# Two recurrent layers: where the gate's mixing product and the per-head mean of the output are computed

## The chip, the core and the metric

The program runs on one core of one Trainium2 chip. The core has five engines that each work through their own queue in order and wait for one another by semaphores: TensorE (PE, matrix products, with weight loads shown apart as PEld), VectorE (DVE), ScalarE (ACT), GpSimd (POOL) and SyncE (SP, which only issues transfers). [...] The metric is the device time of one execution in microseconds (us), as a median over several runs.

## What is computed

Four layers run one after the other on four sequences of 512 rows of 512 channels, all in 32-bit floats: a cross attention, two recurrent layers of the RWKV kind and a last attention with an MLP. The change lies in the two recurrent layers. Cut to what matters, one of them is:

```python
xn = ln(x); sx = shifted(xn) - xn
t  = tanh((xn + sx * maa_x) @ maa_w1).reshape(b, l, 5, 32)
m  = einsum('blfd,fdc->blfc', t, maa_w2)          # five of them: w k v r g
xw, xk, xv, xr, xg = (xn + sx * (maa_j + m_j) for each j)
w  = exp(-exp(time_decay + tanh(xw @ decay_w1) @ decay_w2))
r, k, v = xr @ Wr.T, xk @ Wk.T, xv @ Wv.T ;  g = silu(xg @ Wg.T)
# per head (32 heads of 16 channels), for each row in turn:
#   a = k^T v ; out = r (u * a + s) ; s = a + w * s
gm = mean(y over the 16 channels of a head)
gv = mean((y - gm)**2 over the same)
y  = (y - gm) * rsqrt(gv + eps) * gn_w + gn_b
x  = x + (y * g) @ Wo.T
# then a channel mix of its own (layer norm, two shifted inputs, three products)
```

## The kernel before

**Units.** Each recurrent layer is cut into pieces of 256 rows of one sequence: 2 layers x 4 sequences x 2 halves make 16 units, numbered q. In a unit the recurrence takes eight steps (two halves e of the value channels times four channel groups i). A global step counter g runs over all units, eight steps for each. Products of later units and the output and channel work of earlier ones are laid between the steps, so that three or four units are in work at a time.

**Order.** The order of the instructions on PE, DVE, ACT and POOL is the order in which the program text issues them; nothing rearranges it within these layers. The loop over g issues, at each step: `summed(g-1)` (PE adds up the products of the last step, `py`), `begun(g+1)` (DVE multiplies keys and values into `kv` and `A`, and POOL issues a transfer that adds `A` to `kv` in SBUF), `scan(g)` (the DVE scan along time, and two DVE products `ry`), perhaps `repeated` (PE spreads values into `vr`), and then four phases EARLY, SOON, MID, LATE. Into these phases the generators `mixes(q)`, `outputs(q)` and `channels(q)` put their pieces: a `yield 9, LATE` means "go on in the LATE phase of step 9, counted from the unit's own first step". Within one phase the order is that in which the pieces were registered. At the end of MID every fourth step has `taken`, where DVE adds `py` to half of `y`.

**Buffers.** `A` has one buffer: the product that fills it for step g+1 must wait for the transfer of step g. The small products share three PSUM buffers (tag `p`), the mixing inputs four SBUF buffers (tag `mix`, in turn for `mixx`, `mix_w`, `mix_k`, `mix_v`, `mix_r`, `mix_g`, `ruk`). `mean` and the later `bc` share one.

**The pieces that are touched.** In `mixes`, the helper `second(pair)` computes the second mixing product for one or two of the five letters. For w, k, v, r the weights lie in 32-row strips of one tile; those of g lie in rows 64 to 96 of the tile `dw2`, under the decay's second matrix in rows 0 to 64. `second("g")` is called alone, in the LATE phase of step -5, after `product("k")`; the decay's own second product is in the EARLY phase of step -5. ACT then takes each from PSUM: for g with an Identity and a bias (L665), for the decay with an Exp (L744). `mixed("g")` at step -4, LATE, multiplies by the shift on DVE (L671) and adds the unshifted input by a transfer from POOL (L584).

In `outputs`, the mean over a head's 16 channels starts at step 9, EARLY. The channels of a head lie on four partitions times four slots, and `gmean` is a constant matrix of 1/16 for partitions of one head; four products over the four slots of `y` add up in one PSUM tile, ACT copies it out (L907), and DVE subtracts it (L909). Then come the squares on ACT (L912), the variance on PE (L917) and DVE (L927), its power -1/2 on POOL (L929), and the scaling. What stands next to these in the same phases belongs to other units: at step 8, LATE, that is step 0 of the next unit, where POOL computes `y = v * al` (L799) and `y + rk` (L800) for it.

Of the kernel before, what the change touches and what calls it, by code (L numbers as in the profile page):

```python
# [8 lines left out]
F32 = mybir.dt.float32  # L9
I32 = mybir.dt.int32  # L10
AF = mybir.ActivationFunctionType
ALU = mybir.AluOpType
# [3 lines left out]
P = 128  # L16
B, L, C = 4, 512, 512
KC = C // P
LT = L // P
HS = 16  # L20
TS = 256
BUFS = {"mix": 4, "cx": 3}
# [8 lines left out]
def tile_xattn_rwkv_perceiver(ctx: ExitStack, tc: tile.TileContext, t: dict, out: bass.AP):  # L31
    nc = tc.nc
# [38 lines left out]
    def mm(ps, pairs):  # L71
        for i, (lhsT, rhs) in enumerate(pairs):
            nc.tensor.matmul(ps, lhsT, rhs, start=(i == 0), stop=(i == len(pairs) - 1))  # L73
# [22 lines left out]
    def psum_tile(shape, name):  # L96
        pool, tag = psum["p"]
        return pool.tile(shape, F32, tag=tag, name=name)
# [356 lines left out]
    def recurrent(lp, ep):  # L455
        NI = 4
# [5 lines left out]
        EARLY, SOON, MID, LATE = range(4)  # L462

        mp = sp = pvr = pyp = W = A = None
# [19 lines left out]
        gmean = lp.tile([P, P], F32, name="gmean")  # L484
# [41 lines left out]
        def perm(w, i):  # L526

            return w.rearrange("p (m i) -> p i m", i=NI)[:, i]
# [4 lines left out]
        def pairs(a):  # L533

            return a.rearrange("p i (m o) -> p i o m", o=2)
# [57 lines left out]
        def mixes(q):  # L593
# [5 lines left out]
            c = small[li]  # L599
            vec, order = c["vec"], orders[li]  # L600
# [14 lines left out]
            else:  # L615
                both = wpool.tile([P, 2, KC, TS], F32, tag="w", name="sx0")
                sx, mix = both[:, 0], both[:, 1]
            shift(sx, cur, stT[:, :, b, 1] if hf == 0 else st[q - 1]["last"])
            yield (-10, EARLY) if q == 1 else (-9, LATE)
            if mp:  # L620
                mix = mp.tile([P, KC, TS], F32, tag="mix", name="mixx", bufs=BUFS["mix"])
# [5 lines left out]
            th = lp.tile([P, 2, TS], F32, tag="th", name="th")  # L627
            pm = psum_tile([P, TS], "pm")
            mm(pm, [(c["w1"][:, k, :P], mix[:, k, :]) for k in range(KC)])
            nc.scalar.activation(th[:, 0, :], pm, AF.Tanh)  # L630
            pm = psum_tile([P, TS], "pm")
            for k in range(KC):
# [4 lines left out]
                    start=(k == 0),  # L637
                    stop=(k == KC - 1),
                    tile_position=(0, 64),
                )  # L640
            nc.scalar.activation(th[64:96, 1, :], pm[64:96], AF.Tanh)
            ms = {}

            def second(pair):

                for x in pair:
                    ms[x] = mp.tile([P, KC, TS], F32, tag="mix", name="mix_" + x, bufs=BUFS["mix"])
                for k in range(0, KC, 2):
                    pms = {x: psum_tile([P, 2, TS], "pmm") for x in pair}
                    for a in range(2):  # L650
                        for x in pair:
                            f = order.index(x)
                            r, w = (32 * f, c["w2"]) if f < 4 else (64, c["dw2"])
                            nc.tensor.matmul(
                                pms[x][:, a, :],
                                w[r : r + 32, (k + a) * P : (k + a + 1) * P],
                                th[r : r + 32, f // 4, :],
                                start=True,
                                stop=True,
                                tile_position=(r, 0),  # L660
                            )
                    for x in pair:
                        i = V_MAA + order.index(x)
                        for a in range(2):
                            nc.scalar.activation(  # L665
                                ms[x][:, k + a, :], pms[x][:, a, :], AF.Identity, bias=vec[:, k + a, i : i + 1]
                            )
# [64 lines left out]
            pm = psum_tile([P, TS], "pm")  # L732
            mm(pm[:64], [(c["dw1"][:, k], ms["w"][:, k, :]) for k in range(KC)])
            td = sp.tile([64, TS], F32, tag="td", name="td", bufs=1)
            nc.scalar.activation(td, pm[:64], AF.Tanh)
            mixed("vr")
            yield -5, EARLY
            w = d["w"] = mp.tile(full, F32, tag="o_w", name="o_w", bufs=1)
            for i in range(0, NI, 2):
                pm = psum_tile([P, 2, TS], "pm")  # L740
                for a in range(2):
                    mm(pm[:, a, :], [(perm(c["dw2"][:64], i + a), td)])
                for a in range(2):
                    nc.scalar.activation(  # L744
                        w[:, i + a, :].rearrange("p (o m) -> p o m", o=2),
                        pairs(pm)[:, a],
                        AF.Exp,
                        bias=c["vk"][:, i + a, V_DECAY : V_DECAY + 1],
                    )
            nc.scalar.activation(w, w, AF.Exp, scale=-1.0)  # L750
            yield -5, MID
            product("k")
            yield -5, LATE
            second("g")
            yield -4, MID
            if q > 0:
                product("v")
# [30 lines left out]
            pm = psum_tile([P, TS + TP], "al")  # L788
# [9 lines left out]
            y = d["y"] = mp.tile(full, F32, tag="y", name="y")  # L798
# [97 lines left out]
        def outputs(q):  # L896

            li, b, hf = units[q]
            n = f"L{li}_"
            c, d = small[li], st[q]  # L900
            y = d["y"]
            NQ = TS // 4
            full = [P, NI, TS]
            pm = psum_tile([P, TS], "pmean")
            mm(pm, [(gmean, y[:, i, :]) for i in range(NI)])
            mean = sp.tile([P, TS], F32, tag="mean", name="mean", bufs=1)
            nc.scalar.copy(mean, pm)  # L907
            yield 9, LATE
            nc.vector.tensor_tensor(y, y, mean[:, None, :].to_broadcast(full), ALU.subtract)  # L909
            yield 10, EARLY  # L910
            sq = mp.tile(full, F32, tag="cx", name="sq", bufs=BUFS["cx"])
            nc.scalar.activation(sq, y, AF.Square)  # L912
            yield 10, SOON
            var = psum_tile([P, NQ], "var")
            for i in range(NI):
                for a in range(4):
                    nc.tensor.matmul(  # L917
                        var[32 * a : 32 * a + 32],
                        gm32,
                        sq[:, i, NQ * a : NQ * a + NQ],  # L920
                        start=(i == 0),
                        stop=(i == NI - 1),
                        tile_position=(0, 32 * a),
                    )
            yield 10, LATE
            rstd = sp.tile([P, NQ], F32, tag="gn_rs", name="gn_rs")
            nc.vector.tensor_scalar(rstd, var, 1.0, 1e-5, ALU.mult, ALU.add)  # L927
            yield 11, EARLY
            nc.gpsimd.tensor_tensor(rstd, rstd, mhalf[:, :NQ], ALU.pow)  # L929
            yield 12, LATE  # L930
            for a in range(4):
                rs = slice(32 * a, 32 * a + 32)
                nc.scalar.copy(rp[rs, NQ * a : NQ * a + NQ], rstd[rs])
            yield 13, EARLY
            pm = psum_tile([P, TS], "pbc")
            mm(pm, [(gself, rp)])
            bc = sp.tile([P, TS], F32, tag="mean", name="bc", bufs=1)
            nc.scalar.copy(bc, pm)
            yield 13, LATE
            nc.vector.tensor_tensor(y, y, bc[:, None, :].to_broadcast(full), ALU.mult)  # L940
            yield 14, EARLY

            yg = mp.tile(full, F32, tag="cx", name="yg", bufs=BUFS["cx"])
            for i in range(NI):
                nc.scalar.activation(
                    yg[:, i].rearrange("p (m o) -> p o m", o=2),
                    y[:, i].rearrange("p (o m) -> p o m", o=2),
                    AF.Identity,
                    bias=c["gn"][:, i, 1:2],
                    scale=c["gn"][:, i, 0:1],  # L950
                )
            nc.gpsimd.tensor_tensor(yg, yg, d["g"], ALU.mult)
            yield 15, MID
            wo = wpool.tile([P, NI, C], F32, tag="w", name=n + "wo")
            for a in range(4):
                nc.sync.dma_start(
                    wo[32 * a : 32 * a + 32], t[n + "Wo"].rearrange("(h a i) n -> a h i n", a=4, i=NI)[a]
                )
            pms = []
            for lt in range(NT):  # L960
                pm = psum_tile([P, C], "pm")
                mm(pm, [(yg[:, i, lt * P : (lt + 1) * P], wo[:, i, :]) for i in range(NI)])
                pms.append(pm)
            yield 15, LATE
            for lt in range(NT):
                x = xn[b][hf * NT + lt]
                nc.vector.tensor_tensor(x, pms[lt], x, ALU.add)
# [76 lines left out]
        def follow(q, at, gen):  # L1044
            g, ph = at
            steps.setdefault((G * q + g, ph), []).append((q, gen))

        follow(0, at, first)
        for q in range(len(units)):
            if q > 0:  # L1050
                follow(q, (-13 if q == 1 else -11, LATE), mixes(q))
            follow(q, (9, EARLY), outputs(q))
            follow(q, (19, LATE), channels(q))
        end = G * len(units)
        with (
# [419 lines left out]
```

## Time and profile before

| what | value |
|---|---|
| median of 3 runs | 3840.64 us |
| lowest and highest | 3837.99 and 3846.04 us |
| the profiled execution's own time | 3843.51 us |
| its span, first to last instruction | 3841.5 us |
| instructions in the span | 52407 |
| busy PE, PEld | 3589.6 us (93%), 1900.9 us (49%) |
| busy DVE, ACT, POOL | 2765.4 us (72%), 1691.6 us (44%), 1768.4 us (46%) |
| mean granted PE clock | 0.965 |
| four mean products, all units (L73 pmean) | 128 records, 33.7 us busy on PE |
| the gate's second product, 15 units (L654 pmm<-th,L_dw) | 120 records, 29.8 us |
| the decay's second product, 15 units (L73 pm<-td,L_dw) | 120 records, 33.5 us |
| DVE waiting at L833 for the transfer kv<-A | 88.0 us in 41 waits |
| DVE waiting at L909 for ACT's copy of the mean | 30.8 us in 13 waits |

A product of 32-bit floats shows as two records in the profile, so four products are eight records. The busy time of PE is a union of records that overlap. The recurrent layers fill the stretch from about 760 to 2420 us; the attention layers lie before and after it. An idle time is written in brackets with the instruction that ended it; an engine that is idle is only a cost where it is late for somebody else.

### The profile page before, as it was taken

What the parts mean: (1) busy time and instruction counts of PE and PEld (TensorE: products, weight loads), DVE (VectorE), ACT (ScalarE), POOL (GpSimd) and SP (SyncE); (2) the same over time, 40 slices, a digit from 0 to 9 for tenths busy, and PEclk for the clock granted to TensorE, in tenths of its full rate; (3) what the DMA queues carried; (4) which work ended last, traced back from release to release, by engine and by line L of the source; (5) the groups of instructions that cost most, each with busy time, mean ns of one, the idle gap of its engine ahead of it and who ended that gap; (6) DMA issues with size and microseconds to landing.
All of it is one profiled execution on the core that took longest, in us unless ns stands there. A gap on an engine that the chain in (4) does not pass through costs nothing.

```text
span 3841.5 us, 52407 instructions
## 1 busy us (share of the span) xinstructions
PE 3589.6 (93%) x20544; PEld 1900.9 (49%) x20544; DVE 2765.4 (72%) x4665; ACT 1691.6 (44%) x2514; POOL 1768.4 (46%) x834
## 2 busy tenths in 40 slices
PE   9999999988899999999999967899999999999989
PEld 3333333455565665655665634444454444544446
DVE  6777777689988888888888871388655665667531
ACT  4777676533444444444444422133343334324531
POOL 4777777424444444444444432065533433444430
PEclk9999999989999999999999988899999999999999
DMA  4000000166677777777777754200022122121223
GB/s 149 23 12 23 12 9 20 51 143 133 146 168 176 180 182 171 178 172 167 170 170 171 176 126 129 69 28 17 31 90 70 58 65 71 59 67 36 91 93 121
DMA packets 188805, 386.66 MB, mean 101 GB/s; under 512 B 18128, under 2 KB 44880, under 8 KB 186512
## 3 DMA queue, kind: packets, MB, share of 16 engines
q1 hardware_dynamic: 150256, 251.72, 20.8%
q0 software_dynamic: 38304, 131.61, 18.5%
q8 instruction: 162, 2.65, 0.3%
q14 instruction: 83, 0.68, 0.1%
HBM read 247.50 MB, written 4.19 MB: 66 GB/s over the span
## 4 chain that ended last, share of the span: by engine, by line
PE 64%; DVE 15%; DMA 6%; issue 5%; POOL 5%; ACT 5%; SPq 0%; POOLq 0%; DVEq 0%; ACTq 0%
PE pm L73 9%; PE pv L73 6%; PE po L73 5%; DMA kv<-A 5%; PE ph L73 5%; PE psc L242 5%; PE pst L279 4%; PE pst L1175 3%; PE psc L1175 3%; PE po L304 3%; PE pr L73 3%; DVE ry L867 3%; PE pk L73 3%; PE po L1235 2%; DVE kv L862 2%
## 5 line engine op out<-in xcount | busy, mean ns | idle before, releaser
L1230 POOL TENSOR_TENSOR acc<-acc,aT 128x2048 f32<-128x2048 f32 x96 | 435.0, 4531 | 420.4 <-ACT aT L1225 235.6
L292 POOL TENSOR_TENSOR aT<-aT,nmT 128x1536 f32<-128x1536 f32 x124 | 428.6, 3461 | 206.8 <-ACT aT L290 183.4
L254 DVE CUSTOM_DVE_ANT_0 sc<-psc,nm 128x512 f32<-128x512 f32 x512 | 354.0, 691 | 147.0 <-PE psc L242 89.3
L1220 DVE TENSOR_TENSOR aT<-pst,mb 128x512 f32<-128x512 f32 x512 | 317.4, 681 | 132.0 <-PE pst L1175 132.0
L867 DVE TENSOR_TENSOR ry<-kv,o_r 128x1024 f32<-128x1024 f32 x256 | 347.7, 1398 | 3.5
L862 DVE TENSOR_TENSOR_SCAN kv<-W,kv 128x1032 f32<-128x1032 f32 x128 | 296.1, 2313 | 0.2 <-DMA kv<-A 0.2
L584 POOL DMA_DIRECT2D kv<-A x127 | 118.9, 936 | 379.9 <-DVE kv L839 376.8
L290 ACT COPY aT<-pst 128x512 f32<-128x512 f32 x372 | 196.4, 595 | 178.2 <-PE pst L279 177.7
L298 ACT ACTIVATE aT<-aT 128x2048 f32<-128x2048 f32 x128 | 246.7, 1929 | 5.7 <-POOL aT L292 4.9
L73 PE MATMUL po<-l_m,hT 128*128 128x512 f32 x512 | 237.0, 606 | 9.2 <-ACT hT L1320 9.0
L73 PE MATMUL ph<-nT,l_m 128*128 128x256 f32 x1024 | 240.7, 391 | 0.0
L73 PEld LDWEIGHTS ph<-nT,l_m 128*128 128x128 f32 x1024 | 195.1, 194 | 64.9 <-issue 27.2
L1228 POOL TENSOR_TENSOR acc<-aT 128x2048 f32<-128x2048 f32 x16 | 72.4, 4524 | 327.6 <-ACT aT L1223 327.6
L833 DVE TENSOR_TENSOR A<-vr,o_k 128x1024 f32<-128x1024 f32 x128 | 155.6, 1216 | 88.1 <-DMA kv<-A 88.0
L279 PE MATMUL pst<-q,km 32*128 32x512 f32 x1024 | 206.2, 639 | 9.4 <-DVE mxs L254 5.8
L1189 DVE CUSTOM_DVE_ANT_0 sc<-psc,zeros,mx 128x512 f32<-128x512 f32 x256 | 177.5, 746 | 50.7 <-PE psc L1175 48.4
L1225 ACT ACTIVATE aT<-aT 128x2048 f32<-128x2048 f32 x64 | 122.3, 1911 | 196.6 <-DVE aT L1220 191.6
L1223 ACT ACTIVATE aT<-aT,mc 128x2048 f32<-128x2048 f32 x64 | 128.2, 2003 | 180.3 <-DVE aT L1220 171.0
L242 PE MATMUL psc<-km,q 32*128 32x512 f32 x1024 | 198.8, 653 | 0.8 <-ACT q L223 0.8
L881 PE MATMUL py<-ry,k 128*32 128x512 f32 x1024 | 158.5, 626 | 42.4 <-DVE ry L867 29.6
L929 POOL TENSOR_TENSOR gn_rs<-gn_rs,mhalf 128x64 f32<-128x64 f32 x16 | 186.4, 11648 | 23.0 <-DVE gn_rs L927 23.0
L1189 DVE CUSTOM_DVE_ANT_0 sc<-psc,nm 128x512 f32<-128x512 f32 x256 | 162.9, 686 | 46.5 <-PE psc L1175 45.0
(266 smaller groups left out, 7189.9 us busy)
## 6 DMA issues: line engine op xcount, KB each, us to landing
l_m<-in_L_W SPq DMA_DIRECT2D x64, 1024.0 KB, 5.1
kv<-A POOLq DMA_DIRECT2D x127, 516.0 KB, 7.4
L_wk<-in_L_Wk SPq DMA_DIRECT2D x16, 1024.0 KB, 8.0
L_wr<-in_L_Wr SPq DMA_DIRECT2D x16, 1024.0 KB, 7.8
L_wv<-in_L_Wv SPq DMA_DIRECT2D x16, 1024.0 KB, 6.0
L_wg<-in_L_Wg SPq DMA_DIRECT2D x16, 1024.0 KB, 7.8
L_wo<-in_L_Wo SPq DMA_DIRECT2D x64, 256.0 KB, 7.5
L_fk<-in_L_fWk SPq DMA_DIRECT2D x16, 1024.0 KB, 8.3
```

The lines of the kernel that those rows point to most:

```text
L73: nc.tensor.matmul(ps, lhsT, rhs, start=(i == 0), stop=(i == len(pairs) - 1))
L242: nc.tensor.matmul(psc, d["q"][g][rs, lt * P : (lt + 1) * P], d["km"][rs, a, :], start=True, stop=True, tile_position=(32 * r, 0),)
L254: nc.vector.tensor_tensor_reduce(sc, ps[r], d["nm"][lt], 1.0, -3.0e38, ALU.add, ALU.max, mxs[:, a, lt, c : c + 1])
L279: nc.tensor.matmul(pst, d["km"][rs, a, s * P : (s + 1) * P], d["q2", a][rs, :], start=True, stop=True, tile_position=(32 * r, 0),)
L292: nc.gpsimd.tensor_tensor(w[:, n:, :], w[:, n:, :], nmT[:, None, :].to_broadcast([P, NR - n, L]), ALU.add)
L298: nc.scalar.activation(w, w, AF.Exp)
L862: nc.vector.tensor_tensor_scan(flat(kv), flat(W[g % 2]), flat(kv), 0.0, ALU.mult, ALU.add)
L867: nc.vector.tensor_tensor(y, kv[:, 4 * h : 4 * h + 4, None, :TP].to_broadcast([P, 4, 2, TP]), d["r"][:, i].rearrange("p (o m) -> p o m", o ...
L1175: nc.tensor.matmul(psc, lhsT[rs], rhs[rs], start=True, stop=True, tile_position=(32 * r, 0))
L1189: nc.vector.tensor_tensor_reduce(sc, ps[r], d["nm"][a], 1.0, mx[:, 0, lt, r : r + 1] if a else 3.0e38, ALU.add, ALU.min, mx[:, a, lt, r : ...
L1220: nc.vector.tensor_tensor(w[:, r, :], ps[r], d["mb"][:, r, :], ALU.subtract)
L1230: nc.gpsimd.tensor_tensor(d["acc", m], d["acc", m], w, ALU.add)
```

## The change

Three edits.

First, in `mixes`, the gate's second product is taken out of its own place (step -5, LATE, after the key product) and written into the loop of the decay's second product (step -5, EARLY). For each of two passes there are now two PSUM tiles, `pm` for the decay and `pmm` for the gate, and PE gets a decay product in rows 0 to 64 of the array, then a gate product in rows 64 to 96, twice. ACT takes the decay's two halves, then the gate's two halves, in each pass. The yield at step -5, LATE, is gone with the call; `product("v")`, or `product("r")` in the first unit, stays at step -4, MID.

Second, in `outputs`, POOL adds the four slots of `y` into `mean`, and PE multiplies that sum by `gmean` once. The first add, of the two slots that are complete after step 4, comes at step 6, LATE; the two others at step 8, LATE, after the `taken` of that step; the product stays at step 9, EARLY.

Third, the generator `outputs` is started at step 6, LATE, in place of step 9, EARLY, for that.

In POOL's order the first add follows the scaling and shift of the units before and precedes a kv<-A issue; the two others precede L799 and L800 of the next unit. The orders of DVE and SP are as they were (one of SP's transfers of `wo` changes places with two small weight loads, once), ACT's and PE's differ only in the instructions named.

```diff
+            mg = ms["g"] = mp.tile([P, KC, TS], F32, tag="mix", name="mix_g", bufs=BUFS["mix"])
+            ig = V_MAA + order.index("g")
             for i in range(0, NI, 2):
-                pm = psum_tile([P, 2, TS], "pm")
+                pm, pmg = psum_tile([P, 2, TS], "pm"), psum_tile([P, 2, TS], "pmm")
                 for a in range(2):
-                    mm(pm[:, a, :], [(perm(c["dw2"][:64], i + a), td)])
+                    nc.tensor.matmul(
+                        pm[:, a, :], perm(c["dw2"][:64], i + a), td, start=True, stop=True, tile_position=(0, 0)
+                    )
+                    nc.tensor.matmul(
+                        pmg[:, a, :],
+                        c["dw2"][64:96, (i + a) * P : (i + a + 1) * P],
+                        th[64:96, 1, :],
+                        start=True,
+                        stop=True,
+                        tile_position=(64, 0),
+                    )
...
+                for a in range(2):
+                    nc.scalar.activation(mg[:, i + a, :], pmg[:, a, :], AF.Identity, bias=vec[:, i + a, ig : ig + 1])
             nc.scalar.activation(w, w, AF.Exp, scale=-1.0)
             yield -5, MID
             product("k")
-            yield -5, LATE
-            second("g")
             yield -4, MID
...
+            mean = sp.tile([P, TS], F32, tag="mean", name="mean", bufs=1)
+            nc.gpsimd.tensor_tensor(mean, y[:, 0, :], y[:, 1, :], ALU.add)
+            yield 8, LATE
+            for i in range(2, NI):
+                nc.gpsimd.tensor_tensor(mean, mean, y[:, i, :], ALU.add)
+            yield 9, EARLY
             pm = psum_tile([P, TS], "pmean")
-            mm(pm, [(gmean, y[:, i, :]) for i in range(NI)])
-            mean = sp.tile([P, TS], F32, tag="mean", name="mean", bufs=1)
+            mm(pm, [(gmean, mean)])
             nc.scalar.copy(mean, pm)
...
-            follow(q, (9, EARLY), outputs(q))
+            follow(q, (6, LATE), outputs(q))
```

## The prediction

> **What bounds the kernel now.** The page gives 93% to PE and 72% to DVE over the whole span. The change touches the recurrent layers only, so I read the busy time there, in hundreds of microseconds (columns: stretch, its length, then busy us and instruction count of PE, PEld, DVE, ACT, POOL, the granted clock, DMA share, GB/s).
>
> ```profile
> 1600.00:1700.00 100.00, 94.95 (x647) 60.40 (x649) 87.40 (x91) 46.36 (x92) 46.45 (x32) 1.00 0.73 169
> ```
>
> PE leads, but DVE is only 7 us behind. An average of that kind cannot say which of two engines paces, so I took the timeline of one unit (half a batch of one layer, eight scan steps, about 98 us). First VectorE (start, duration, operation, and in brackets its idle time and what ended it):
>
> ```profile
> 1631.35 4.33 DVE L867 TENSOR_TENSOR ry<-kv,o_r 128x1024 f32<-128x1024 f32 x2
> 1636.21 0.68 DVE L894 TENSOR_TENSOR y<-py,y 128x512 f32<-128x512 f32 x1
> 1636.81 1.21 DVE L833 TENSOR_TENSOR kv<-vr,o_k 128x1024 f32<-128x1024 f32 x1
> 1637.94 1.21 DVE L833 TENSOR_TENSOR A<-vr,o_k 128x1024 f32<-128x1024 f32 x1
> 1639.07 0.16 DVE L839 COPY kv<-S 128x8 f32<-128x8 f32 x1
> 1639.14 2.29 DVE L862 TENSOR_TENSOR_SCAN kv<-W,kv 128x1032 f32<-128x1032 f32 x1
> 1641.47 2.36 DVE L867 TENSOR_TENSOR ry<-kv,o_r 128x1024 f32<-128x1024 f32 x2
> 1645.15 1.23 DVE L909 TENSOR_TENSOR y<-y,mean 128x1024 f32<-128x1024 f32 x1 [1.32 <-ACT mean L907]
> 1649.70 1.22 DVE L833 TENSOR_TENSOR A<-vr,o_k 128x1024 f32<-128x1024 f32 x1
> 1658.18 0.23 DVE L927 TENSOR_SCALAR gn_rs<-var 128x64 f32<-128x64 f32 x1 [0.32 <-PE var L917]
> 1681.04 0.69 DVE L894 TENSOR_TENSOR y<-py,y 128x512 f32<-128x512 f32 x1 [3.94 <-PE py L881]
> 1688.01 1.22 DVE L833 TENSOR_TENSOR A<-vr,o_k 128x1024 f32<-128x1024 f32 x1 [4.01 <-DMA kv<-A]
> ```
>
> DVE waits for PE three times: 1.32 us before the subtraction of the mean, 0.32 us for the variance, 3.94 us at L894. The third is worth nothing: two instructions later DVE waits 4.01 us more for the kv<-A transfer, whose issue stands on POOL behind the power of L929:
>
> ```profile
> 1629.97 3.49 POOL L799 TENSOR_TENSOR y<-o_v,al 128x1024 f32<-128x1024 f32 x1
> 1636.43 1.27 POOL L800 TENSOR_TENSOR y<-y,rk 128x512 f32<-128x512 f32 x1 [2.96 <-DVE rk L794]
> 1639.53 0.87 POOL L584 DMA_DIRECT2D kv<-A  x1 [1.83 <-DVE kv L839]
> 1661.61 11.72 POOL L929 TENSOR_TENSOR gn_rs<-gn_rs,mhalf 128x64 f32<-128x64 f32 x1
> 1677.13 1.53 POOL L584 DMA_DIRECT2D kv<-A  x1
> ```
>
> So in this unit the pace is: PE up to the variance, then power, transfer and DVE until the next unit. DVE has no bracket over 0.6 us between 1688 and the next 1.5 us wait for the mean at 1744. In 4 of the 12 middle units (their gate step at 1027, 1127, 1321 and 1417 us) DVE waits 2.9 to 3.8 us for ACT o_g at L717; ACT there follows PE's receptance product, so PE paces those units throughout. In the first units (before 1000 us) DVE has no wait for the mean.
>
> The PE rows that the change touches:
>
> ```profile
> 1642.72 1.99 PE L73 MATMUL pmean<-y,gmean 128*128 128x256 f32 x8
> 1667.98 2.23 PE L73 MATMUL pm<-td,L_dw 64*128 64x256 f32 x8
> 1677.91 1.99 PE L654 MATMUL pmm<-th,L_dw 32*128 32x256 f32 x8
> ```
>
> **Mean, on PE.** Four products (8 records) become one. The step from pmean's start to the next row's is 1.92 us; a quarter stays, 0.48, so 1.44 us goes per unit, ahead of the variance and hence on PE's path.
>
> **Mean, on POOL.** Three adds of 128x256 appear. Price: L1230 adds 128x2048 in 4531 ns, L800 adds 128x512 in 1272 ns; the line through both is 187 ns + 2.12 ns per element, so 0.73 us each. Below nothing it cannot be; if the cost did not shrink from 512 elements it is 1.27. I take 0.73. The first add stands in POOL's order behind the shift of L588/L589 and ahead of a kv<-A issue that idles 2.1 us for DVE (3.8 in other units): hidden. The other two are put ahead of L799 and L800 of the next unit, which in turn stand ahead of the kv<-A issue at 1639.53. And they wait for L894, so everything behind them on POOL now begins at L894's end.
>
> **What that wait does to DVE.** Row first: while L799 runs, DVE's ry pair takes 4.33 us; the next pair takes 2.36. Here L799 costs DVE 1.97 us. [...] L833 reads vr from PSUM and keeps its 1.21 us everywhere. [...] the two adds fall beside the two L833.
>
> Count from L894's end (t). L799 no longer runs beside ry, so t comes 1.97 us earlier than before. Adds 0.15 to 1.6. L799 takes 2.38 us (its undisturbed minimum), 1.6 to 4.0. DVE's two L833 last to 2.27, then the copy L839 is held to 4.0. L800 takes its turn, to 5.4 (in the trace the engines alternate: L589, queued behind L588, waits for one ry and not for two). Scan 5.4 to 7.7, ry to 9.95. Against the old t that is 7.98; before, L909 began at 8.26. So DVE is held 2.9 us where it was held 1.97, and the 1.32 us wait for the mean is gone: 0.28 us gained. ACT's mean copy is then ready some 0.9 us earlier (the W copy before it becomes the limit), and PE, which reaches pmean 5.8 us after the old t, finds the adds long done. PE's variance is 1.44 us earlier, so the 0.32 us wait falls too: **0.6 us per unit** where DVE and POOL pace. The kv<-A issue moves from 2.63 to 3.5 after the old t; a landing takes 7.4 us, so at 1647.8, before 1649.4 when the next A wants the buffer. That transfer costs nothing, with 1.6 us left.
>
> **Gate beside the decay, on PE.** Eight records of the gate leave their place between key and value products and are laid between the decay's eight. Nearest row: the other maa pair (L654, two row groups interleaved) takes 1.56 + 1.13 us and a wait of 0.59 for ACT to free one of three PSUM buffers, 3.2 us in all; the new step has the same four tiles, buffers and waits. Before: 2.16 + 1.92 = 4.08. I take 3.4, the decay's strided weights being slower to load, so 0.7 us goes. [...] the other end is a loss of 0.6, if nothing overlaps and the wait comes on top. All of it lies after the variance, beside the power and the 11 us transfer, so it counts only in PE-paced units. ACT does the same evacuations, four of them earlier, before exp; nothing reads o_w for over 20 us. Should that cover go, it is under 2 us per unit. mix_g takes mix_w's buffer, already read. DVE's order is unchanged.
>
> **Sum.** Eight DVE-paced units: 8 x 0.6 = 4.8. Four PE-paced: 4 x (1.44 + 0.7) = 8.6, DVE's wait at L717 leaving room. Three early units without a wait to remove: about +0.9 each for two of them, -1.9 in all. Last unit, where pmean stands in the chain of waits: 1.4. First, where the gate's products do: 0.7. Together 13.6 us from the profiled run's 3843.5: 3829.9. That run lies 2.9 above the median of 3840.64, so I forecast **3827**; its own range, adds at 0.55 to 0.9 us, is 3818 to 3836. 0.2%, or 7.7 us, is about what a measurement can tell from no change.
>
> **Rivals.**
> 1. PE paces everywhere (for: its 95%; against: DVE's waits for transfers). Fifteen units at 2.1 us less: 3840.6 - 32 = 3809.
> 2. Slower: the adds hold POOL. If two adds take over 2.27 us (1.1 each), DVE's scan starts before L799 gets its turn. Then with 1.27 each: adds to 2.7, scan to 4.7, L799 to 7.1, one ry, L800 to 9.6, and kv<-A is issued 9.7 after t, 5.1 later than before. It lands near 1652; A comes 2.3 us late, the variance wait gives 0.3 back. Twelve units at 2.0: 3865.
> 3. No change: the scan goes before L800. kv<-A is issued 3.0 us later, lands at 1650, and A is 0.3 late, which eats the variance's 0.3: 3840.
>
> Chances: forecast 0.50, rival 1 0.18, rival 2 0.18, rival 3 0.14. Faster takes three quarters of the forecast, all of rival 1 and a little of 3: 0.60. Slower is rival 2 and a little of 3: 0.20. The range runs 3803 to 3855, leaving out the far ends of rivals 1 and 2.
>
> **What would show it.** An add near 0.73 us; ry at step 8 back to 2.4 and the next copy or scan held; no bracket at L909; kv<-A in step 9 issued 3.5 us after the old t without a wait at L833 behind it; decay and gate together near 3.4 us. A wait for DMA kv<-A at that L833 is rival 2 or 3. PE idle ahead of pmean would refute me in any form.

## The result and the profile after

| | before | after |
|---|---|---|
| median, 15 runs each | 3842.73 us | 3853.93 us |
| lowest and highest | 3836.16 and 3854.25 | 3845.83 and 3858.19 |
| profiled execution, span | 3841.5 us | 3850.6 us |
| time at half clock in it | 268 us | 343 us |

The ratio is 1.0023, with a 95% interval of 1.0012 to 1.0034 (the two medians alone give 1.0029): slower by a little more than a measurement can tell, where faster was forecast. The forecast of 3827 is missed by 27 us; the time lies at the far end of the range, on the other side of no change. That the range holds it is luck: its upper part was there for a rival (the adds hold POOL) that did not come about.

The time at half clock is summed from the granted-clock intervals of the trace. But for one that is cut off, every such interval is a whole number of windows of 3.41 us long, on one fixed grid, and the clock in it is 0.50; such a window is called a half window below. (Up to 2.4 us of these sums lie behind the last instruction.)

The same hundred microseconds of the recurrent layers as before (columns as there):

```profile
1600.00:1700.00 100.00, 96.17 (x676) 59.65 (x672) 86.05 (x91) 45.03 (x90) 46.77 (x33) 0.98 0.75 175
```

PE is busier than before (96.17 against 94.95), DVE less (86.05 against 87.40), and the granted clock is 0.98 where it was 1.00. The page's chain of waits points the same way for the whole span; its line by engine after the change:

```profile
PE 70%; DVE 12%; ACT 6%; POOL 5%; issue 5%; DMA 2%; SPq 0%; POOLq 0%; DVEq 0%; ACTq 0%
```

Before, PE had 64%, DVE 15% and DMA 6% of it. So the kernel did not become bound by GpSimd or a transfer; it is bound by PE in more places than before, although the change takes products away from PE. Two places show how.

**The mean.** Timeline of one unit after the change, step 8 and 9, DVE, POOL and PE together. The line numbers have moved: L907, L927, L812, L813, L852, L875 and L880 here are L894, L909, L799, L800, L839, L862 and L867 of the kernel before.

```profile
1646.56 2.36 DVE L880 TENSOR_TENSOR ry<-kv,o_r 128x1024 f32<-128x1024 f32 x2
...
1649.43 0.68 DVE L907 TENSOR_TENSOR y<-py,y 128x512 f32<-128x512 f32 x1
...
1650.27 1.54 POOL L921 TENSOR_TENSOR mean<-mean,y 128x256 f32<-128x256 f32 x2 [4.79 <-DVE y L907]
...
1651.76 2.35 POOL L812 TENSOR_TENSOR y<-o_v,al 128x1024 f32<-128x1024 f32 x1
1652.30 1.85 DVE L852 COPY kv<-S 128x8 f32<-128x8 f32 x1
1654.06 2.29 DVE L875 TENSOR_TENSOR_SCAN kv<-W,kv 128x1032 f32<-128x1032 f32 x1
1654.19 3.22 POOL L813 TENSOR_TENSOR y<-y,rk 128x512 f32<-128x512 f32 x1
1657.36 0.86 POOL L584 DMA_DIRECT2D kv<-A  x1
...
1657.92 0.70 PE L73 MATMUL pmean<-mean,gmean 128*128 128x256 f32 x2
...
1659.55 1.21 DVE L927 TENSOR_TENSOR y<-y,mean 128x1024 f32<-128x1024 f32 x1
```

The two adds take 1.54 us behind L907, the first ry pair is at 2.36 us, L852 (0.17 us in the median) is held to 1.85 us, until L812 ends, and L927 has no bracket. All of this is as forecast but for one turn: DVE's scan goes before POOL's L813, not after it. L813 then takes 3.22 us (1.27 where it is shortest) and the kv<-A issue comes at 1657.36, 7.25 us after the end of L907.

**The gate beside the decay.** PE's timeline in the same unit (start, duration; x2 is one product):

```profile
1681.89 0.84 PE L745 MATMUL pm<-td,L_dw 64*128 64x256 f32 x2
1682.65 0.69 PE L748 MATMUL pmm<-th,L_dw 32*128 32x256 f32 x2
1683.28 0.83 PE L745 MATMUL pm<-td,L_dw 64*128 64x256 f32 x2
1684.04 0.69 PE L748 MATMUL pmm<-th,L_dw 32*128 32x256 f32 x2
...
1686.06 0.83 PE L745 MATMUL pm<-td,L_dw 64*128 64x256 f32 x2
1686.82 0.96 PE L748 MATMUL pmm<-th,L_dw 32*128 32x256 f32 x2
1687.72 8.98 PE L73 MATMUL pm<-mix_k,L_wk 128*128 128x256 f32 x32
```

The starts step by 0.76 and 0.63 us in turn. No product starts beside its neighbour, and each takes longer than it did in a block of its own (0.54 and 0.48): from the first decay product to the key product it is 5.83 us, where the two blocks took 4.08 together. A half window begins at 1687.1 and stretches the last gate product; in the six units where none reaches into the pair it takes 5.56, in others up to 7.67. Then the key product, 7.84 us before, takes 8.98. The third view, busy time by stretches, has the granted clock (the third number from the right):

```profile
1676.00:1681.80 5.80, 5.80 (x24) 2.24 (x22) 5.73 (x8) 0.80 (x2) 5.80 (x2) 1.00 1.06 210
1681.90:1687.70 5.80, 5.80 (x20) 3.31 (x16) 5.17 (x8) 2.75 (x7) 5.80 (x2) 0.95 0.70 224
1687.70:1696.00 8.30, 8.30 (x31) 7.77 (x31) 2.49 (x3) 2.44 (x5) 4.08 (x5) 0.83 0.71 129
```

PE is busy without a gap in all three, and yet the clock falls behind the alternation, to 0.83 in the last.

### The profile page after: what moved, and what is told of

Its sections match the earlier page's. It is cut to its first block, busy times and chain, and to the rows that moved or that the text cites. A ratio compares the mean times of both kernels' runs of the same rounds, so it can differ in the third digit from the quotient of the medians.

```text
span 3850.6 us, 52289 instructions
## 1 busy us (share of the span) xinstructions
PE 3631.5 (94%) x20448; PEld 1896.9 (49%) x20448; DVE 2745.1 (71%) x4665; ACT 1686.5 (44%) x2514; POOL 1794.6 (47%) x882
## 4 chain that ended last, share of the span: by engine, by line
PE 70%; DVE 12%; ACT 6%; POOL 5%; issue 5%; DMA 2%; SPq 0%; POOLq 0%; DVEq 0%; ACTq 0%
PE pm L73 11%; PE pv L73 6%; PE po L73 5%; PE ph L73 5%; PE psc L242 4%; PE pst L279 4%; PE pst L1193 3%; PE psc L1193 3%; PE pr L73 3%; PE po L304 3%; PE pm L689 3%; PE pk L73 3%; PE po L1253 2%; DVE ry L880 2%; DVE aT L1238 2%
## 5 line engine op out<-in xcount | busy, mean ns | idle before, releaser
L880 DVE TENSOR_TENSOR ry<-kv,o_r 128x1024 f32<-128x1024 f32 x256 | 353.8, 1423 | 4.0
L875 DVE TENSOR_TENSOR_SCAN kv<-W,kv 128x1032 f32<-128x1032 f32 x128 | 296.3, 2315 | 0.2 <-DMA kv<-A 0.2
L894 PE MATMUL py<-ry,k 128*32 128x512 f32 x1024 | 162.8, 628 | 40.9 <-DVE ry L880 30.2
L1193 PE MATMUL pst<-q,kT 32*128 32x512 f32 x1024 | 181.7, 645 | 5.2 <-DVE mx L1207 4.3
```

The lines of the kernel that those rows point to most:

```text
L875: nc.vector.tensor_tensor_scan(flat(kv), flat(W[g % 2]), flat(kv), 0.0, ALU.mult, ALU.add)
L880: nc.vector.tensor_tensor(y, kv[:, 4 * h : 4 * h + 4, None, :TP].to_broadcast([P, 4, 2, TP]), d["r"][:, i].rearrange("p (o m) -> p o m", o ...
L1193: nc.tensor.matmul(psc, lhsT[rs], rhs[rs], start=True, stop=True, tile_position=(32 * r, 0))
```

## The experiments

The first question was which half of the change costs; the second, what in the alternation costs; the third, why the mean brings nothing. Each run's ratio is against the kernel before on the same chip. Diffs are against the changed kernel and show the part that the text speaks of: a run with the block behind the decay has gate_after_decay's gate beside it, one with equal heights that of gate_64rows.

| run | mean | gate | us, median | ratio, 95% interval |
|---|---|---|---|---|
| mean_only | GpSimd | late, as before | 3844.95 | 1.0007 (0.9998 to 1.0016) |
| gate_only | PE | alternating | 3870.48 | 1.0075 (1.0059 to 1.0091) |
| gate_after_decay | GpSimd | block behind the decay | 3814.76 | 0.9941 (0.9919 to 0.9963) |
| gate_64rows | GpSimd | alternating, equal heights | 3819.31 | 0.9937 (0.9923 to 0.9951) |
| gate_moved_only | PE | block behind the decay | 3821.90 | 0.9937 (0.9921 to 0.9954) |
| gate_64rows_only | PE | alternating, equal heights | 3827.11 | 0.9950 (0.9938 to 0.9961) |
| gate_pairs | GpSimd | two and two | 3828.12 | 0.9956 (0.9943 to 0.9969) |
| mean_four | GpSimd, 4 products | block behind the decay | 3824.96 | 0.9962 (0.9950 to 0.9974) |
| mean_two | GpSimd, 2 products | block behind the decay | 3819.67 | 0.9948 (0.9937 to 0.9960) |
| mean_three | GpSimd, 3 products | block behind the decay | 3821.15 | 0.9944 (0.9923 to 0.9965) |
| gate_64rows_two | GpSimd, 2 products | alternating, equal heights | 3809.29 | 0.9909 (0.9886 to 0.9931) |
| gate_64rows_three | GpSimd, 3 products | alternating, equal heights | 3821.12 | 0.9947 (0.9929 to 0.9965) |

### The two halves

mean_only is the changed kernel with the gate as before:

```diff
-                pm, pmg = psum_tile([P, 2, TS], "pm"), psum_tile([P, 2, TS], "pmm")
+                pm = psum_tile([P, 2, TS], "pm")
...
             product("k")
+            yield -5, LATE
+            second("g")
```

> Only the mean's half of the change; gate and decay products as before. If the loss sits in the gate's half (both theories of it), the decay takes 2.2 us and the gate 2.0 us again, the key product 7.8 us at full clock, and the time falls to 8 to 14 us below before (3829 to 3835). If the mean's half carries the loss (POOL late, kv<-A late), the time is at or above before.

The gain expected for a loss in the gate's half did not come: nothing that can be told from no change. So the mean wins nothing by itself either; more on that below.

gate_only is the kernel before with the first edit alone:

```diff
-            nc.gpsimd.tensor_tensor(mean, y[:, 0, :], y[:, 1, :], ALU.add)
...
-            mm(pm, [(gmean, mean)])
+            mm(pm, [(gmean, y[:, i, :]) for i in range(NI)])
...
-            follow(q, (6, LATE), outputs(q))
+            follow(q, (9, EARLY), outputs(q))
```

> Only the gate's half of the change; the mean by four products as before. If the gate's half carries the loss: decay and gate together 5.6 to 5.8 us instead of 4.1, then some us at half clock in the key product, 2.7 us more per unit on PE, of which the waits of PE for DVE take up a part: 15 to 30 us above before. If the loss were the mean's, this kernel would be at or below before.

As expected, 27 us slower. With gate_after_decay, the next run, it shows that the alternation is what makes the change slower; the mean wins some of it back beside it (1.0075 to 1.0023).

### What in the alternation costs

gate_after_decay keeps everything of the change but the alternation:

```diff
-                pm, pmg = psum_tile([P, 2, TS], "pm"), psum_tile([P, 2, TS], "pmm")
+                pm = psum_tile([P, 2, TS], "pm")
...
+            second("g")
             nc.scalar.activation(w, w, AF.Exp, scale=-1.0)
             yield -5, MID
             product("k")
```

> The whole change, but the four gate products follow the four decay products instead of alternating with them: same place, same work, same PSUM tiles, one change of tile height in place of seven. Theory 1 [...]: 4.1 to 4.6 us for both, key product 7.8 us at full clock, time like mean_only, 8 to 14 us below before. Theory 2 (the decay's strided weights load slowly and cannot be hidden behind another tile): also about 4.1 us, so this run does not tell the two apart; it tells whether alternating is what costs. If the cost were the place (ACT or PSUM), it would stay above before.

It was far better than expected, 28 us below before instead of 8 to 14. The blocks take 2.16 and 1.92 us again. The key product takes 7.84 in seven of the sixteen units; in the others it is 9.35 to 9.44, so half windows remain behind the block.

gate_64rows keeps the alternation, and fills the gate's weights and inputs up with zero rows from 32 to 64:

```diff
+            nc.gpsimd.memset(dw2[96:, :], 0.0)
...
-                        c["dw2"][64:96, (i + a) * P : (i + a + 1) * P],
-                        th[64:96, 1, :],
+                        c["dw2"][64:, (i + a) * P : (i + a + 1) * P],
+                        th[64:, 1, :],
```

> The whole change, with the gate's product made 64 rows high (rows 96 to 128 of weights and inputs are zeros), so that both tiles have one height and still alternate. Theory 1 (tiles of unlike height don't overlap): the pairs overlap, 3.0 to 3.6 us for all eight, no half clock behind them, time at or below mean_only. Theory 2 (strided weights): nothing changes against the change itself, 5.6 to 5.8 us, half clock, about 10 us above before.

PE's timeline of gate_64rows, the first rows of the pair, its one wait, and what follows:

```profile
1652.03 0.60 PE L748 MATMUL pm<-td,L_dw 64*128 64x256 f32 x1
1652.03 0.70 PE L751 MATMUL pmm<-th,L_dw 64*128 64x256 f32 x2
...
1654.26 0.48 PE L751 MATMUL pmm<-th,L_dw 64*128 64x256 f32 x1 [0.46 <-ACT o_w L760]
...
1655.32 7.84 PE L73 MATMUL pm<-mix_k,L_wk 128*128 128x256 f32 x32
```

The two products start at the same time, and all eight take 3.29 us with a wait of 0.46 in it; the key product takes 7.84 in all sixteen units. The decay's weights are read with the same stride as in the changed kernel, and one load of them takes about as long (0.33 us in the median, there 0.32; the gate's 0.19 and 0.18), so stride is not the cause: the equal heights overlap here (3.29 us), the unequal ones there don't (5.56).

gate_pairs has two decay products, then two gate products, in turn:

```diff
                     nc.tensor.matmul(
                         pm[:, a, :], perm(c["dw2"][:64], i + a), td, start=True, stop=True, tile_position=(0, 0)
                     )
+                for a in range(2):
                     nc.tensor.matmul(
                         pmg[:, a, :],
```

> As the changed kernel, but two decay products and then two gate products in turn, so the height of the tile changes 7 times instead of 15 between first and last product. Theory 1 (each change of height costs the same, about 0.11 us: 1.6 us over 15 changes): decay and gate together 4.7 to 4.9 us instead of 5.6 to 5.8, and the kernel between the changed one (3854) and gate_after_decay (3815): 3825 to 3842 us. Theory 2 (it is not the change of height but the alternation of two accumulator tiles, or a price that does not depend on the count): 5.4 us or more, and 3848 to 3860 us.

PE's timeline of gate_pairs (x4 is two products):

```profile
1670.63 1.30 PE L745 MATMUL pm<-td,L_dw 64*128 64x256 f32 x4
1671.86 1.13 PE L749 MATMUL pmm<-th,L_dw 32*128 32x256 f32 x4
1672.92 1.30 PE L745 MATMUL pm<-td,L_dw 64*128 64x256 f32 x4
1674.15 1.13 PE L749 MATMUL pmm<-th,L_dw 32*128 32x256 f32 x4
1675.21 7.84 PE L73 MATMUL pm<-mix_k,L_wk 128*128 128x256 f32 x32
```

4.58 us for three changes of height inside, against 4.08 for the two blocks, which have one, and 5.56 at full clock for the alternation's seven. Counted so, a change of height costs 0.25 us, the first two and the next four alike (0.50 and 0.98). The expectation had counted 7 and 15 changes where there are 3 and 7, and so put one at 0.11 us; measured, the pair is 0.1 to 0.3 us under its band. The time fell between its two neighbours, as theory 1 had it.

### The place of the gate, and the mean

gate_moved_only is gate_after_decay with the mean as before, gate_64rows_only is gate_64rows with it:

```diff
-            mm(pm, [(gmean, mean)])
+            mm(pm, [(gmean, y[:, i, :]) for i in range(NI)])
...
-            follow(q, (6, LATE), outputs(q))
+            follow(q, (9, EARLY), outputs(q))
```

> The mean as in the kernel before, on TensorE; of the gate only the place is changed: its four products in a block of their own straight after the decay's four, before the key product, no alternation. Theory 1 (the place alone makes the gain that gate_after_decay showed, because one thin stretch of 32-row products fewer stands between the large products): 3812 to 3825 us. Theory 2 (either part alone only moves the wait: the mean's 1.44 us on TensorE and the gate's place must be changed together, since each alone leaves the other's wait): 3836 to 3848 us, the same as before. In the trace the pair of blocks takes 4.1 us and no product of the key runs at half clock behind it.

> The mean as in the kernel before; the gate's products alternate with the decay's, but both on 64 rows (the gate's weights filled up with zero rows), so no tile height changes. Theory 1 (products of equal height on different rows do overlap, and that saving reaches the end without the mean's part): 3812 to 3828 us, with decay and gate together in 3.3 us. Theory 2 (both parts are needed): 3836 to 3848 us with the same 3.3 us in the trace. With gate_64rows at 3819 the difference of the two is what the mean on GpSimd is worth beside a gate that overlaps.

Theory 1 held in both: the new place alone gives 23 us, the new place with the products beside each other 18. The intervals of the two ratios share most of their width, so the 0.8 us per unit that laying the products beside each other takes off PE (3.29 against 4.08) cannot be seen in the time.

Where the place gains can be read from the kv<-A transfer behind the power. L_wo, 1 MB in four parts, takes a buffer that the key product frees (in the kernel before, SP waits at L956 for PE's pm 12 times, 146.4 us in all). There, L_wo is issued 0.9 us after kv<-A (at 1677.13); kv<-A then lands after 10.9 us, and DVE waits 4.01 us at 1688.01:

```profile
1670.14 7.84 PE L73 MATMUL pm<-mix_k,L_wk 128*128 128x256 f32 x32
1678.01 2.88 SPq L956 DMA_DIRECT2D L_wo<-in_L_Wo  x4
```

In gate_moved_only the gate's 1.92 us stand ahead of the key product, L_wo comes 2.2 us after kv<-A, and kv<-A lands after 7.7:

```profile
1659.39 1.99 PE L654 MATMUL pmm<-th,L_dw 32*128 32x256 f32 x8
1661.31 7.84 PE L73 MATMUL pm<-mix_k,L_wk 128*128 128x256 f32 x32
1667.02 1.54 POOL L584 DMA_DIRECT2D kv<-A  x1
1669.18 3.37 SPq L957 DMA_DIRECT2D L_wo<-in_L_Wo  x4
1674.70 1.23 DVE L834 TENSOR_TENSOR A<-vr,o_k 128x1024 f32<-128x1024 f32 x1 [1.45 <-DMA kv<-A]
```

The same transfer in eleven middle units, us:

| run | L_wo after kv<-A, mean | kv<-A to its landing, mean | DVE idle ahead of the next A, sum |
|---|---|---|---|
| before | 0.79 | 10.39 | 40.1 |
| mean_only | 0.58 | 10.75 | 46.4 |
| gate_moved_only | 2.91 | 7.48 | 7.4 |
| gate_after_decay | 3.44 | 7.46 | 4.0 |
| gate_64rows | 2.08 | 8.73 | 28.7 |
| changed kernel | 6.13 | 6.54 | 0.0 |

Over all fourteen kernels, the 25 such transfers with L_wo less than 1.5 us behind them took 10.9 us in the mean, the 119 with 2 us or more 7.2. In gate_moved_only DVE's wait is 3.0 us per unit shorter than before, and the unit 2.6 (95.62 against 98.22). The table also fits that missing gain: with the shorter pair (3.29 us against 4.08) the key product ends sooner, L_wo comes closer to kv<-A again (2.08 against 3.44), and part of the wait is back (28.7 against 4.0). No run moved L_wo alone, so this is read from the traces, not tested.

With the gate well placed, the mean on GpSimd is worth nothing that these ratios can tell, though it takes 1.3 us per unit off PE, which is by then 96% busy. Over ten units in the middle, gate_moved_only takes 95.62 us per unit and gate_after_decay 95.59 (from copy of the mean to copy of the mean). The half windows can account for the 1.3: none in these units of gate_moved_only, 3.07 us per unit in gate_after_decay. Of these nine, five stand behind the mean and four behind the gate's block. gate_after_decay, PE's timeline behind the mean:

```profile
1634.82 1.07 PE L883 MATMUL py<-ry,k 128*32 128x512 f32 x8
1635.82 0.70 PE L73 MATMUL pmean<-mean,gmean 128*128 128x256 f32 x2
1636.45 1.59 PE L654 MATMUL pmm<-th,L_w 32*128 32x256 f32 x10
1638.50 1.45 PE L654 MATMUL pmm<-th,L_w 32*128 32x256 f32 x6 [0.47 <-ACT mix_v L665]
1639.88 8.46 PE L73 MATMUL pr<-L_fr,xr 128*128 128x512 f32 x16
```

The receptance product takes 8.46 us, and the clock from 1638.9 to 1642.3 is 0.54. Between two large products lie products on 32 rows (L654) and on 32 columns (L883) of the array, and the mean's product is the only one there that fills it.

mean_four tests this: four products on PE again, with the adds left on GpSimd:

```diff
-            mm(pm, [(gmean, mean)])
-            nc.scalar.copy(mean, pm)
+            mm(pm, [(gmean, mean) for i in range(NI)])
+            nc.scalar.activation(mean, pm, AF.Copy, scale=0.25)
```

mean_two sums three planes on GpSimd, mean_three two (it has no second GpSimd statement at all). mean_two:

```diff
-            for i in range(2, NI):
-                nc.gpsimd.tensor_tensor(mean, mean, y[:, i, :], ALU.add)
+            nc.gpsimd.tensor_tensor(mean, mean, y[:, 2, :], ALU.add)
...
-            mm(pm, [(gmean, mean)])
+            mm(pm, [(gmean, mean), (gmean, y[:, 3, :])])
```

mean_three:

```diff
-            yield 8, LATE
-            for i in range(2, NI):
-                nc.gpsimd.tensor_tensor(mean, mean, y[:, i, :], ALU.add)
...
-            mm(pm, [(gmean, mean)])
+            mm(pm, [(gmean, mean), (gmean, y[:, 2, :]), (gmean, y[:, 3, :])])
```

> As gate_after_decay (mean summed on GpSimd, the gate's block behind the decay's), but the product of the sum is issued four times and the copy out of its accumulator scales by a quarter, so TensorE has the mean's four products back and GpSimd keeps its three adds. Theory 1 (taking three of the four products away is what brings a 3.4 us window at half clock per unit behind that place; it gives back the 1.44 us): with four products the windows at half clock behind the mean go, a unit takes 95.4 to 95.9 us as in gate_after_decay and gate_moved_only, and the time is 3812 to 3823 us. Theory 2 (the window at half clock has nothing to do with these products): the window stays, a unit takes 1.4 us more than in gate_after_decay, 97.1 us, and the time is 3832 to 3842 us.

> As gate_after_decay, but only three of the four planes are summed on GpSimd (one add fewer behind the last), and the product is issued twice, on the sum and on the fourth plane: TensorE has 0.48 us more per unit. Theory 1 (the clock holds again once enough products of 128 rows stand in that stretch): if two suffice, the window at half clock goes and a unit takes 94.4 to 94.9 us, the time 3794 to 3806 us; if two do not suffice, 96.1 us and 3818 to 3828. Theory 2 (clock unconnected): 96.1 us and 3818 to 3828 us as well, but then mean_four keeps the window too.

> As gate_after_decay, but only the first two planes are summed on GpSimd (no add behind the last take) and the product is issued three times: on the sum and on the third and fourth planes. With one and with two products a window at half clock stood behind that place, with four none. If three are enough, the window goes and a unit takes 95.5 less 0.48, 95.0 us: 3808 to 3818 us, by 4 to 8 below mean_four. If they are not, a unit takes 96.5 us and the time is 3824 to 3832.

PE's timeline of mean_four at the same place:

```profile
1639.93 1.07 PE L883 MATMUL py<-ry,k 128*32 128x512 f32 x8
1640.93 1.99 PE L73 MATMUL pmean<-mean,gmean 128*128 128x256 f32 x8
1642.86 1.56 PE L654 MATMUL pmm<-th,L_w 32*128 32x256 f32 x10
1644.91 1.13 PE L654 MATMUL pmm<-th,L_w 32*128 32x256 f32 x6 [0.50 <-ACT mix_v L665]
1645.97 7.13 PE L73 MATMUL pr<-L_fr,xr 128*128 128x512 f32 x16
```

The receptance product takes 7.13 us, at full clock, and between 1089 and 2090 us the clock falls twice only, against ten times in gate_after_decay. Three products that compute nothing new keep the clock up here, and cost about what they save: the times of the two kernels can't be told apart. A unit takes 95.4 to 95.9 us through most of the middle, as theory 1 had it; the median of 3825 is 2 us above its band, but below theory 2's. With three products the median of 3821 lies between its two branches: the half window comes in every third unit (periods 95.0, 95.0, 96.7 in turn), with two in nearly every one, there or behind the gate (96.32 us per unit, theory 1's second branch). So it is a matter of degree.

gate_64rows_two and gate_64rows_three join the two findings; their edits are that of gate_64rows with that of mean_two or of mean_three.

> As gate_64rows (gate beside decay on equal tile heights), with the mean as in mean_two. Theory 1: half its units had a 3.4 us window at half clock and took 95.1 us, the others 93.4; with two products and no such window all would take 93.9, 1 us less than now on the mean, so 3806 to 3814 us; if two products do not suffice, 3820 to 3828 us. Theory 2: 3820 to 3828 us.

> As gate_64rows (gate beside decay on 64 rows each), with the mean as in mean_three. If three products hold the clock, no window stands behind the mean, and a unit takes what gate_64rows took in its units without a window, 93.4, and 0.96 us more: 94.4 us, 3804 to 3813 us. If not, 96 us and 3818 to 3828. It is also the candidate for the fastest version, beside gate_64rows_two at 3809.

gate_64rows_two is the lowest median of all, 0.9909 of the kernel before; but its runs spread from 3786 to 3818 us, and its half windows did not go (2.73 us per unit), so the first branch's time was met without its reason, and the rank over gate_64rows is not settled. gate_64rows_three missed its first branch: half windows in more than half of its units, 3821 us.

### One account of all

The clock in a half window is 0.50, so I estimate what the full clock would have saved at half of that time, at most (1.71 us per window; the key product of gate_after_decay takes 1.5 to 1.6 us more in the units where a half window is left behind the block). Taken off the span, what is left is a rough measure of the rest (one profile of each):

| profiled run | span | at half clock | span less half of it |
|---|---|---|---|
| before | 3841.5 | 268 | 3707 |
| changed kernel | 3850.6 | 343 | 3679 |
| mean_only | 3849.5 | 324 | 3687 |
| gate_only | 3879.7 | 357 | 3701 |
| gate_moved_only | 3809.7 | 247 | 3686 |
| gate_after_decay | 3809.5 | 298 | 3660 |
| mean_four | 3819.2 | 255 | 3692 |
| gate_64rows | 3814.7 | 292 | 3669 |
| gate_pairs | 3826.3 | 336 | 3658 |

On this account the mean is worth 20 to 26 us wherever it is made (before to mean_only 20, gate_only to changed 22, gate_moved_only to gate_after_decay 26), near 16 x 1.3 = 21. The alternation costs 15 to 19 against the block, where 16 x 1.5 would be 24. Two rows don't fit. gate_64rows has less on PE than gate_after_decay, and 9 us more is left; DVE's wait for kv<-A in the table above is longer there. gate_pairs has 16 x 0.5 = 8 us more on PE, and 2 less is left. And before to gate_moved_only leaves 21 with the same products on PE: that is the place. So the account is good to some 10 us. The changed kernel is 28 us better than before in it, and loses up to 37 by its clock.

## Why the prediction was wrong

- **An add at 0.73 us; ry at 2.36; no wait for the mean**: right. **Mean on PE, 1.44 us**: nearly; the one product left takes 0.63 us from its start to the next row's, not 0.48, so 1.3 came off. The sum behind the 0.28 us slips by 0.1: a scan that ends at 7.7 and a ry pair of 2.36 make 10.06, not 9.95. Nothing below turns on it.
- **"L800 takes its turn, to 5.4"**: wrong in the order; the scan went first, as in the third rival. The kv<-A issue came 5.3 us after the old t, not 3.5. In the changed kernel it cost nothing, because DVE was not what the unit waited for: DVE's waits for kv<-A between 1000 and 2200 us, 69.0 us in all before, are a fifth of that in the view of waits of the changed kernel (who waits for whom, us in all, times, longest):

```profile
DVE A L846 <- DMA kv<-A: 14.8, 9, 5.6
```

- **The second rival** (adds hold POOL) fell: the adds took 1.54 us together, under its 2.27.
- **"I take 3.4" for gate and decay together, with "a loss of 0.6" as the worst end**: this step failed. It measured 5.56 at full clock, so 1.5 us lost per unit in place of 0.7 won. The row it rested on, the other maa pair, has two tiles of 32 rows; the step puts 64 beside 32. The wait for ACT that the worst end was made of did not come at all; what came was a price for the change of height, which neither end held: about 0.25 us for each change, worked out from the two blocks, gate_pairs and the alternation (4.08, 4.58 and 5.56 us). What PE does in that time was not shown.
- **"It counts only in PE-paced units", beside "the 11 us transfer"**: this failed too. The 11 us were taken as fixed, but the gate's place sets when L_wo joins that transfer (0.79 us behind it before, 6.13 in the changed kernel); in the changed kernel it landed in 6.5 us and DVE's wait for it was gone. That was a gain that the sum did not hold. With the alternation and the clock, PE paced all the middle units: DVE waits 12 times for ACT at L717 in them, 47.5 us in all.
- **No term for the clock**: put at nothing without a word. The changed kernel spends 75 us more at half clock, up to 37 us of time. In its trace a half window stands behind the alternation in each middle unit, and one behind the mean in most, where three of four products are gone. The two don't add up: gate_only, with all four, has 357 us of it.
- **The first rival** (PE paces everywhere, 3809) had the right engine and a wrong sign, since PE got more to do, not less.

What stays open: in gate_moved_only the half time per middle unit also goes from 3.41 us to none, and how much of the 23 us is due to that and how much to the shorter transfer was not separated. Nor was it in mean_only: its half time in ten middle units is 4.8 us per unit where it was 3.4, at other places of the unit than the mean's own in part, and its wait for kv<-A is longer too (46.4 against 40.1); either may hold what the mean won.

## What to carry to other kernels

Before laying small products side by side on PE, look whether they take the same number of rows (here 64 beside 32 took 5.56 us, 64 beside 64 3.29, two blocks 4.08); if not, fill the smaller up with zeros or keep them in blocks (in time the two were worth the same, 0.9937 and 0.9941). Taking a product off PE may win nothing if the stretch it leaves fills too little of the array (between 1089 and 2090 us the clock fell ten times with one mean product, twice with four, and the times could not be told apart): look for what stands around it, and count the half-clock time of both traces before explaining a difference. A transfer's time is not fixed (kv<-A took 10.9 us with L_wo close behind it, 7.2 without): ask which other transfer the change will start beside it. A row of the trace is near only if it is alike in what sets the price, here the tile's height (the row had 32 beside 32 and took 3.2 us, the step 64 beside 32 and took 5.56).

## What the runs showed of the hardware

**What stands before a half window.** In these runs PE's busy share did not tell when the clock fell. For every full-clock window between 1100 and 2130 us of the two kernels and the twelve experiments, I added up PE's products, each weighted by the share of the array it uses (rows/128 times columns/128) and by the time a product on the whole array takes for its length (0.24 us per record of 256 columns, from the mean's eight records in 1.92 us), as a share of the window's 3.41 us. Of 121 windows that a half window followed, 119 lie at 0.42 or less; of 3955 that none followed, 9 do. By busy share the two kinds can't be parted: the median of the first is 0.86, and 705 of the others lie below it. In the changed kernel the window inside the alternation comes to 0.25 to 0.29 while PE is busy all through. So how much of the array was at work parts the two kinds here, and how busy PE was does not; what sets the clock was not shown. The weights are my own working, the 0.42 was chosen on these same windows and tried on no others, and a few per cent of the records may be missing.

**A unit that fits the grid.** In ten middle units, gate_after_decay, gate_moved_only, mean_three, gate_64rows_two and gate_64rows_three take 95.52 to 95.62 us per unit, although their products on PE differ by more than a microsecond; 28 windows are 95.57 us (an interval of 563.20 us in the trace before is 165 of them). A shorter unit would move its thin stretches along the grid until one fills a window and the clock pays the difference back, as the 95.0, 95.0, 96.7 of mean_three may do. But over ten units that begin one later, the five spread from 95.63 to 96.16, and gate_moved_only has no half window there at all. So this is a conjecture, and was not tested.
